# Front products of a transformer block in seven-for-eight form, and expert lists kept in DRAM

## The chip, the cores and the metric

The kernel runs on one core of one Trainium2 chip. The metric is the device time of one execution in microseconds (us): 1033.31 us as the median of 3 runs (1033.22 to 1034.61). A core has five engines with a queue of instructions each: TensorE (PE), VectorE (DVE), ScalarE (ACT), GpSimd (POOL) and SyncE (SP), which issues most DMA transfers. POOL issues the indirect ones (gathers and scatters by a list of rows).

## The reference

Sixteen sequences of 512 tokens with 256 features pass through one block, all in float32:

```python
xn = _layernorm(x, axis=-1)
x = x + attention(xn) + experts(xn)
# attention: 16 heads of 16, linear (no softmax over tokens)
q, k = elu(xn @ Wq + bq) + 1, elu(xn @ Wk + bk) + 1;  v = xn @ Wv + bv
kv = einsum('bkhd,bkhm->bhdm', k, v)
out = einsum('bqhd,bhdm->bqhm', q, kv) / max(sum over tokens of q.k, 1e-6) @ Wo + bo
# experts: one shared, and 2 of 8 routed
shared = swiglu(xn @ w_in.T) @ w_out.T
g = the better of 2 groups by softmax(xn @ wg.T + gb)
e_logits = xn @ we.T + eb, softmax inside group g; the best two of its 4 experts
h = swiglu(xn @ w1.T)                      # 512 wide, common to all experts
routed = sum over the two of weight * (h @ w2[e].T)
```

The two experts of a token are in the same group of four, so a token has one of 12 pairs.

## The kernel before, in words

**Sequences.** The loop over `b` handles one sequence of 512 tokens (4 tiles of 128) in an iteration. It also runs the front of sequence b+1 and the normalization of sequence b+2. In PE's order an iteration is: `project` of b+1 (k with the 8 + 2 logits beside it, 8 products of 266 columns on line 412, then q, 8 of 256 on line 423), `summarize` of b (L689, keys against normalized inputs), `hidden_rows` of b (L595, h in token rows, sent to `h_d` in DRAM), `key_sum` of b+1 (L679), `hidden` of b (L621, the shared expert's hidden values), the small `values` and `mix` (L708, L731), and `gather` (L768, the shared expert and attention outputs added to the residual `res`, also sent to `h_d`).

**Seven products for eight.** `hidden_rows` and `hidden` compute a 2 by 2 block product with 7 block products. `weight_sums` (L527) makes four sums of weight blocks once, `token_sums` (L538 to L541) four sums of the token blocks of each sequence, from the transposed input `xnT`. `seven` walks 14 products (7 for each of 2 halves `u`) through three PSUM banks a half, called tall, wide and lone; between products ACT copies a bank out and DVE adds others to it. A product that continues a bank waits for that copy.

**Order.** Each engine has one fixed order, made by a scheduler from the order of the text, priorities and its own estimate of times; `keep_in_program_order`, `issue_after` and `high_priority` steer it. PSUM is split into 6 banks for `ps_mm` and 2 for `ps_y`. Tiles with the same tag share buffers. SP's transfers also go out in one order.

**Front.** After the products DVE adds the biases (L416, L417, L427), `feature_map` makes elu + 1 with an exponential on ACT (L398 to L402), and `route` finds the pair of each token (L446 to L515): `hot` marks it, `ahead_of` counts, on POOL, the tokens of each pair in the same partition in earlier tiles. `attend` divides the queries by their normalizer and sends them through DRAM to be transposed (`turn`, L258 and L264).

**Sorting.** After the front of sequence 15, `order` sorts all 8192 tokens by pair into tiles of 128, each tile of one pair. It turns counts into slots, and then makes, for 8 groups of 8 token tiles, one-hot marks on DVE (L877 to L890) that 64 bfloat16 products on PE (L894) sum to the list of tokens of each tile. The result is `source` and `goal` (L921, L923). `between` runs these steps piece by piece between the products of sequences 14 and 15.

**Routed experts.** There are at most 75 tiles; 67 are done always, the rest under a condition on the count. Two tiles make a pair of tiles. `rows` (L943) gathers rows of `h_d`, 770 values each: 512 of h, 256 of the base (residual, attention and shared expert) and two weights. `turn` (L964 to L976) transposes h, `sums` multiplies by the two experts' weights (L993), adds weights and base (L1000, L1003), and scatters the rows to the output (L1006). The gathered rows live in four homes, the memory of qq_all, x_all, kk_all and xn_all. The first three pairs of tiles are gathered early for h (L943 at 768 us), and once more after the last residual rows are in `h_d`.

## Time and profile before

| | before |
|---|---|
| median of 3 runs | 1033.31 us |
| profiled execution | 1033.23 us |
| its span, first to last instruction | 1031.5 us |
| PE busy / DVE / ACT / POOL | 1004.9 / 779.4 / 488.1 / 254.8 us |
| granted PE clock, mean | 0.998 |

The profile records one execution. A row of a group gives line, engine, operation and tiles, a count, then busy time and mean duration. A float32 matrix product shows as two records. Durations of PE records overlap, so the distance between starts is what a product costs in a full queue. In rows in order of time, the bracket at the end gives idle time before the instruction and what released it. Time stamps are us from the start of the span.

### The profile page before, as it was taken

What the parts mean: (1) busy time and instruction counts of PE and PEld (TensorE: products, weight loads), DVE (VectorE), ACT (ScalarE), POOL (GpSimd) and SP (SyncE); (2) the same over time, 40 slices, a digit from 0 to 9 for tenths busy, and PEclk for the clock granted to TensorE, in tenths of its full rate; (3) what the DMA queues carried; (4) which work ended last, traced back from release to release, by engine and by line L of the source; (5) the groups of instructions that cost most, each with busy time, mean ns of one, the idle gap of its engine ahead of it and who ended that gap; (6) DMA issues with size and microseconds to landing.
All of it is one profiled execution on the core that took longest, in us unless ns stands there. A gap on an engine that the chain in (4) does not pass through costs nothing. (4 is left out here: it accounts for less than half of the span.)

```text
span 1031.5 us, 12407 instructions
## 1 busy us (share of the span) xinstructions
PE 1004.9 (97%) x3704; PEld 681.7 (66%) x3704; DVE 779.4 (76%) x1974; ACT 488.1 (47%) x893; POOL 254.8 (25%) x359
## 2 busy tenths in 40 slices
PE   7999999999999999999999999999899999999996
PEld 5466868677786868686777768686667344444442
DVE  5978687878778787878787877868975776666663
ACT  3525353535445253535343534425136576766671
POOL 5302020111202021110202020201012766555652
PEclk9999999999999999999999999999999999999999
DMA  7063534525152522314141313221235755555440
GB/s 220 16 177 107 141 104 101 147 59 154 51 163 54 161 84 81 122 42 143 37 128 56 110 55 123 72 77 61 62 110 146 225 172 153 147 156 157 150 147 30
DMA packets 130339, 116.08 MB, mean 113 GB/s; under 512 B 72637, under 2 KB 114109, under 8 KB 130272
## 3 DMA queue, kind: packets, MB, share of 16 engines
q1 hardware_dynamic: 120064, 77.43, 25.7%
q0 software_dynamic: 9392, 37.58, 12.2%
q8 instruction: 31, 0.51, 0.2%
q10 hardware_dynamic: 816, 0.27, 0.2%
q14 instruction: 36, 0.29, 0.1%
HBM read 65.36 MB, written 50.27 MB: 112 GB/s over the span
## 5 line engine op out<-in xcount | busy, mean ns | idle before, releaser
L993 PE MATMUL py<-w_sb,hT 128*128 x536 | 230.7, 592 | 1.7 <-DVE hT L976 1.6
L993 PEld LDWEIGHTS py<-w_sb,hT 128*128 128x128 f32 x536 | 101.7, 190 | 130.1 <-issue 129.1
L768 PE MATMUL po<-wout_sb,hs_all 128*128 128x256 f32 x480 | 116.6, 380 | 1.4 <-DVE hs_all L580 1.4
L390 POOL TENSOR_TENSOR res<-x_all,bo_sb 128x256 f32<-128x256 f32 x64 | 48.5, 792 | 274.4 <-DMA h_d<-res 203.4
L768 PEld LDWEIGHTS po<-wout_sb,hs_all 128*128 128x128 f32 x480 | 89.2, 190 | 15.1 <-DVE hs_all L580 3.4
L1006 POOL DMA_INDIRECT out<-y,goal x67 | 67.8, 1012 | 76.3 <-DVE y L1003 65.3
L676 POOL TENSOR_TENSOR k<-kk_all 128x512 f32<-128x512 f32 x16 | 20.9, 1307 | 258.3 <-DVE sm L458 247.7
L777 DVE TENSOR_TENSOR res<-po,res 128x256 f32<-128x256 f32 x60 | 25.4, 424 | 76.6 <-PE po L768 76.5
L398 ACT ACTIVATE km<-km 128x1024 f32<-128x1024 f32 x16 | 16.9, 1057 | 138.7 <-DVE km L397 134.4
L595 PE MATMUL phr_w<-w_sb,ss 128*128 128x512 f32 x120 | 61.5, 594 | 2.2 <-DVE ss L538 1.9
L768 PE MATMUL po<-kvo,qT 128*128 128x256 f32 x240 | 61.7, 383 | 0.0
L621 PE MATMUL phs_w<-ss,win_sb 128*128 128x256 f32 x240 | 61.6, 379 | 0.0
L621 PE MATMUL phs_t<-xnT,win_sb 128*128 128x256 f32 x240 | 61.6, 379 | 0.0
L595 PE MATMUL phr_t<-w_sb,xnT 128*128 128x512 f32 x120 | 61.3, 593 | 0.0
L595 PE MATMUL phr_t<-w_sb,ss 128*128 128x512 f32 x120 | 59.4, 597 | 0.0
L621 PE MATMUL phs_t<-ss,win_sb 128*128 128x256 f32 x240 | 59.1, 379 | 0.0
L689 PE MATMUL pxk<-kk_all,xn_all 128*128 128x256 f32 x256 | 58.0, 379 | 0.0
L412 PE MATMUL pk<-wkr_sb,xnT 128*128 128x266 f32 x240 | 57.2, 387 | 0.0
L423 PE MATMUL pq<-w_sb,xnT 128*128 128x256 f32 x240 | 54.2, 379 | 0.0
L689 PEld LDWEIGHTS pxk<-kk_all,xn_all 128*128 128x128 f32 x256 | 48.5, 190 | 6.7 <-issue 0.2
L964 ACT COPY hb<-qq_all 32x256 f32<-32x256 f32 x108 | 43.4, 402 | 17.1 <-DMA qq_all<-h_d,source 9.7
L412 PEld LDWEIGHTS pk<-wkr_sb,xnT 128*128 128x128 f32 x240 | 45.4, 190 | 8.0
(216 smaller groups left out, 1966.0 us busy)
## 6 DMA issues: line engine op xcount, KB each, us to landing
h_d<-hr SPq DMA_DIRECT2D x64, 256.0 KB, 2.5
q_d<-qq_all SPq DMA_DIRECT2D x16, 512.0 KB, 2.8
qb<-q_d SPq DMA_DIRECT2D x64, 128.0 KB, 3.1
w_sb<-in_w SPq DMA_DIRECT2D x64, 128.0 KB, 3.5
h_d<-res SPq DMA_DIRECT2D x60, 129.0 KB, 1.9
x_all<-in_x SPq DMA_DIRECT2D x15, 512.0 KB, 4.8
xn_d<-xn_all SPq DMA_DIRECT2D x14, 512.0 KB, 3.9
xb<-xn_d SPq DMA_DIRECT2D x56, 128.0 KB, 2.8
```

The costliest lines, as they stand in the source:

```text
L390: nc.gpsimd.tensor_tensor(res[:, t, 0:D], xt[:, t, :], bo_sb, ALU.add)
L412: nc.tensor.matmul(pk, lhsT=xnT[:, k, ts(t, P)], rhs=wkr_sb[:, k, :], start=(k == 0), stop=(k == KD - 1),)
L423: nc.tensor.matmul(pq[:, t, :], lhsT=xnT[:, k, ts(t2 + t, P)], rhs=wq_sb[:, k, :], start=(k == 0), stop=(k == KD - 1),)
L595: tc.keep_in_program_order(nc.tensor.matmul(to, lhsT=xs7[i][:, ts(u, P)], rhs=w1_in[W7[i]], start=start, stop=stop, skip_group_check=True,))
L621: tc.keep_in_program_order(nc.tensor.matmul(split(to)[:, f, :], lhsT=win_in[W7[i]][:, ts(2 * u + f, P)], rhs=xs7[i], start=start and f == ...
L676: nc.gpsimd.tensor_tensor(k2, kk[:, 0:2, :], kk[:, 2:4, :], ALU.add)
L689: nc.tensor.matmul(pxk[:, c, :], lhsT=xn[:, t, ts(c, P)], rhs=kk[:, t, :], start=(t == 0), stop=(t == NT - 1),)
L768: nc.tensor.matmul(po, lhsT=a, rhs=w, start=(i == 0), stop=(i == len(parts) - 1))
L777: nc.vector.tensor_tensor(res[:, t, 0:D], po, res[:, t, 0:D], ALU.add)
L964: nc.scalar.copy(there[ts(q, Q), a - near, 0:n, :], self.hg[ts(a, Q), 0:n, ts(q, W)])
L993: nc.tensor.matmul(py.rearrange("p j d -> p (j d)"), lhsT=self.hT[:, f, ts(j, P)], rhs=w2_sb[:, f, bass.ds(regs[i % TR], 2 * D)], start=(f ...
L1006: stored = nc.gpsimd.indirect_dma_start(out=out_rows, out_offset=bass.IndirectOffsetOnAxis(ap=self.goal[:, i : i + 1], axis=0), in_=y, in_ ...
```

## The change

**Front products.** From sequence 2 on `project7` replaces `project`. It computes k and q together by 14 products of 261 columns: the k side has 256 columns of k, the four logits of group 0 and its group logit, the q side the same with group 1. ACT copies and DVE adds take the results out of PSUM. The query bias is then added by DVE and the key bias by POOL. `token_sums` runs at the end of the iteration before and serves `project7`, `hidden_rows` and `hidden`. The weight blocks `kq_sb` are loaded at the start, completed with the logit columns by POOL copies (`by_side`) and summed by DVE (`weight_sums`) in iteration 0.

**Lists.** `clear_lists` fills a list in DRAM for each pair in iteration 0 (780 rows of 4096 bytes). `enlist` finds, for each sequence, each token's place in its pair's list with two bfloat16 products, and scatters the token numbers, one entry of 32 bytes for a token, with four scatters. `order` is reduced to the counts; it gathers the tiles' lists from DRAM with one gather and transposes them on PE. The marks, their 64 products and `between` go.

**Rows.** A row has 771 values: h, weights, base, and one of padding. Thus its last third (257 values) is a row of its own for `bases`, which fetches the final base for the first three pairs instead of a second whole gather. `hs_all` becomes a fifth home, and rows are gathered four pairs ahead. Buffers of kvo, y and ss have new tags. `values` and `mix` of sequence 14 are placed between the products of `hidden`, as those of sequence 15, and its outputs start with the attention part.

```diff
-    BASE = D + 2
...
+    BASE = 2 + D + 1
     ROW = HID + BASE
+    LAST = D + 1
...
+    kq_sb = wp.tile([P, SEVEN, SIDE], FP)
+    kq_in = [kq_sb[:, i, :] for i in range(SEVEN)]
+    kq_12 = w2_sb[:, 0, 2 * D : 2 * D + SIDE]
+    nc.sync.dma_start(out=kq_sb[:, 0:KD, 0:D], in_=wk.rearrange("(p c) f -> p c f", p=P))
+    for k, to in enumerate((kq_12, kq_in[2])):
+        nc.sync.dma_start(out=to[:, 0:D], in_=wq.rearrange("(p c) f -> p c f", p=P)[:, k])
+    bl_sb = const.tile([P, G, EL], FP)
+    def by_side():
+        for g, y in enumerate((kq_in[0:2], (kq_12, kq_in[2]))):
+            for to, rows in [*((y[k], wkr_sb[:, k]) for k in range(KD)), (None, bkr_sb)]:
+                to = bl_sb[:, g, :] if to is None else to[:, D:SIDE]
+                nc.gpsimd.tensor_copy(to[:, 0:EG], rows[:, D + g * EG : D + (g + 1) * EG])
+                nc.gpsimd.tensor_copy(to[:, EG:EL], rows[:, D + E + g : D + E + g + 1])
...
         res = work.tile([P, NT, BASE], FP, tag="res", name=f"res_{b}")
         xt = xs.pop(b)
         for t in range(NT):
-            nc.gpsimd.tensor_tensor(res[:, t, 0:D], xt[:, t, :], bo_sb, ALU.add)
+            nc.gpsimd.tensor_tensor(res[:, t, 2 : 2 + D], xt[:, t, :], bo_sb, ALU.add)
+        nc.gpsimd.memset(res[:, :, 2 + D :], 0.0)
         return res
...
+    def project7(b, xs7):
+        sides = [a[:, b % 2] for a in (kk_all, qq_all)]
+        kk, qq = sides
+        tall, wide, lone = [None] * 2, [None] * 2, [None] * 2
+        for u in range(2):
+            tall[u], wide[u], lone[u] = (
+                ps_mm.tile([P, SIDE], FP, tag="mm", name=f"pkq_{b}_{u}_{i}") for i in "twl"
+            )
+        for u, i in (
+            (0, 1), (0, 5), (1, 1), (0, 6), (1, 5), (1, 6), (0, 7), (0, 2), (1, 7), (0, 4), (1, 2),
+            (0, 3), (1, 4), (1, 3),
+        ):
+            to = lone[u] if i == 2 else wide[u] if i in (3, 5) else tall[u]
+            tc.keep_in_program_order(nc.tensor.matmul(
+                to, lhsT=xs7[i - 1][:, ts(u, P)], rhs=kq_in[W7[i - 1]],
+                start=i in (1, 2, 5), stop=i in (2, 3, 4), skip_group_check=True,
+            ))
+            a1, b1, a2, b2 = kk[:, u, :], qq[:, u, :], kk[:, 2 + u, :], qq[:, 2 + u, :]
+            with tc.high_priority():
+                if i in (1, 6, 7, 4):
+                    last_copy[:] = [nc.scalar.copy({1: a1, 6: b1, 7: b2, 4: a2}[i], tall[u])]
+                if i in (7, 2, 3):
+                    c, p = {7: (b2, wide[u]), 2: (a1, lone[u]), 3: (b1, wide[u])}[i]
+                    nc.vector.tensor_tensor(c, c, p, ALU.add)
+        lg = small.tile([P, NT, G * EL], FP, tag="lg", name=f"lg_{b}")
...
+        for y, bias, tag, engine in (
+            (qq, bq_sb, "qm", nc.vector), (kk, bkr_sb[:, 0:D], "km", nc.gpsimd),
+        ):
+            engine.tensor_tensor(
+                y[:, :, 0:D], y[:, :, 0:D], bias.unsqueeze(1).to_broadcast([P, NT, D]), ALU.add
+            )
+            feature_map(b, y, tag)
+        return qq[:, :, 0:D], kk[:, :, 0:D], lg
...
+    def clear_lists():
+        free = work.tile([P, P * WORDS], U32, tag="blocks", name="free")
+        nc.gpsimd.memset(free, FREE)
+        R = lists_d.shape[0]
+        for r in range(0, R, P):
+            n = min(P, R - r)
+            nc.sync.dma_start(out=lists_d[r : r + n, :], in_=free[0:n, :])
...
+    def enlist(b):
+        pr = ps_y.tile([P, NT, NP], FP, tag="py", name=f"pr_{b}")
+        flat = pr.rearrange("p t c -> p (t c)")
+        mine = hot[:, ts(b, NT), :]
+        nc.tensor.matmul(flat, lhsT=before, rhs=mine.rearrange("p t c -> p (t c)"), start=True, stop=False)
+        nc.tensor.matmul(
+            flat, lhsT=ones_bf, rhs=ahead_of[:, ts(b, NT), :].rearrange("p t c -> p (t c)"),
+            start=False, stop=True,
+        )
+        rk = small.tile([P, NT, NP], FP, tag="rk", name=f"rk_{b}")
+        nc.vector.tensor_tensor(rk, pr, lists_at.unsqueeze(1).to_broadcast([P, NT, NP]), ALU.add)
+        nc.vector.tensor_tensor(rk, rk, mine, ALU.mult)
+        rf = small.tile([P, NT], FP, tag="rf", name=f"rf_{b}")
+        nc.vector.tensor_reduce(rf, rk, AX.X, ALU.add)
+        spot = small.tile([P, NT], U32, tag="spot", name=f"spot_{b}")
+        nc.vector.tensor_scalar(spot, rf, float(WORDS), None, ALU.mult)
+        for t in range(NT):
+            put = nc.gpsimd.indirect_dma_start(
+                out=entries,
+                out_offset=bass.IndirectOffsetOnAxis(ap=spot[:, t : t + 1], axis=0),
+                in_=ids[:, b * NT + t : b * NT + t + 1], in_offset=None,
+            )
+            tc.declare_no_dep(put.ins, group="lists", reason="every token has an entry of its own")
+            tc.add_to_no_dep_group("lists", put.ins)
...
         (x11, x12), (x21, x22) = halves(xnT)
-        ss = one.tile([P, 4, S // 2], FP, tag="ss", name=f"ss_{b}")
...
-        if b + 1 == B:
+        if b + 2 >= B:
...
-        with tc.high_priority() if b + 1 == B else nullcontext():
+        kvo = one.tile([P, KD, D], FP, tag="xk", name=f"kvo_{b}")
+        with tc.high_priority() if b + 2 >= B else nullcontext():
...
             nc.tensor.matmul(po, lhsT=a, rhs=w, start=(i == 0), stop=(i == len(parts) - 1))
         return po
...
+        past = keep.tile([P, NP - 1], FP)
+        nc.vector.tensor_scalar(past, starts[:, 1:], row, None, ALU.is_le)
+        nc.vector.tensor_tensor(past, past, jump[:, 0 : NP - 1], ALU.mult)
+        begin = keep.tile([P, 1], FP)
+        nc.vector.tensor_reduce(begin, past, AX.X, ALU.add)
+        part = keep.tile([P, 1], U32)
+        nc.vector.tensor_scalar(part, begin, row, 1.0 / P, ALU.add, ALU.mult)
+        got = work.tile([P, P * WORDS], U32, tag="blocks", name="got")
+        nc.gpsimd.indirect_dma_start(
+            out=got[0:TILES, :], out_offset=None, in_=lists_d,
+            in_offset=bass.IndirectOffsetOnAxis(ap=part[0:TILES, :], axis=0),
+        )
+        tokens = keep.tile([P, P], FP)
+        nc.vector.tensor_copy(
+            tokens[0:TILES, :], got[0:TILES, :].rearrange("p (n w) -> p n w", w=WORDS)[:, :, 0]
+        )
         yield
...
-        def marks(g):
-            row_of, tile_of = (place_of[:, i, ts(g, TG)].unsqueeze(2) for i in range(2))
-            lo, hi = los[:, g % 4], his[g % 3]
-            nc.vector.tensor_tensor(
-                lo, count.unsqueeze(1).to_broadcast([P, TG, P]), row_of.to_broadcast([P, TG, P]),
-                ALU.is_equal,
-            )
-            at_tile = one.tile([P, TG, TILES], BF, tag="at_tile", name=f"at_tile_{g}")
-            nc.vector.tensor_tensor(
-                at_tile, count[:, 0:TILES].unsqueeze(1).to_broadcast([P, TG, TILES]),
-                tile_of.to_broadcast([P, TG, TILES]), ALU.is_equal,
-            )
-            nc.vector.tensor_tensor(
-                hi[:, :, 0, :], at_tile,
-                number[:, ts(g, TG)].unsqueeze(2).to_broadcast([P, TG, TILES]), ALU.mult,
-            )
-            nc.vector.tensor_scalar(hi[:, :, 1, :], at_tile, row, None, ALU.mult)
...
-        def add(g):
-            for t in range(TG):
-                tc.keep_in_program_order(nc.tensor.matmul(
-                    pi, lhsT=los[:, g % 4, t, :], rhs=his[g % 3][:, t].rearrange("p i n -> p (i n)"),
-                    start=(g + t == 0), stop=(g * TG + t == TT - 1),
-                ))
...
+        pi = ps_y.tile([P, TILES], FP, tag="py", name="pi")
+        nc.tensor.transpose(pi, tokens[0:TILES, :], ident[0:TILES, 0:TILES])
...
+        def bases(self):
+            for j, i in enumerate(self.tiles):
+                nc.gpsimd.indirect_dma_start(
+                    out=self.hg[:, j, HID + 2 :], out_offset=None,
+                    in_=h_d.rearrange("r (a w) -> (r a) w", w=LAST),
+                    in_offset=bass.IndirectOffsetOnAxis(ap=lasts[:, i : i + 1], axis=0),
+                )
...
         res = residual(b)
-        qq, kk, lg = project(b, xnT)
-        route(b, lg, res)
+        qq, kk, lg = project7(b, sums7[b]) if b in sums7 else project(b, xnT)
...
-            steps_of_order = order()
         if b + 1 == B:
-            sums7 = token_sums(b, xnT)
-            hidden_rows(b, sums7, {2: 2, 6: 2, 9: 2, 13: 2}.get)
+            hidden_rows(b, sums7[b])
             for e in waiting:
                 load_expert(e)
-            *lists, filled = next(steps_of_order)
             tiles = [Tiles(list(range(i, min(i + 2, SURE))), *lists) for i in range(0, SURE, 2)]
+            lasts = keep.tile([P, 2 * AHEAD], U32)
+            parts = ROW // LAST
+            nc.vector.tensor_scalar(
+                lasts, lists[0][:, 0 : 2 * AHEAD], float(parts), float(parts - 1), ALU.mult, ALU.add
+            )
...
         if b + 1 < B:
             sums = key_sum(b + 1, fronts[b + 1][2])
             queries[b + 1] = attend(b + 1, fronts[b + 1][1], sums)
-        if b + 2 == B:
-            next(steps_of_order)
+        if 0 < b < B - 1:
+            enlist(b + 1)
         if b + 1 == B:
             for w in tiles[:AHEAD]:
                 w.rows()
-        if b + 1 < B:
-            hs, made = hidden(b, sums7) if b else first_hidden(xnT)
+        if b + 2 < B:
+            hs, made = hidden(b, sums7[b]) if b else first_hidden(xnT)
+            if b == 0:
+                clear_lists()
+                by_side()
+                for _ in weight_sums(kq_in, kq_12):
...
             made_of = {}
-            hs, made = hidden(b, sums7, then)
+            hs, made = hidden(b, sums7[b], then)
             kvo = made_of["kvo"]
-        if b + 2 == B:
-            next(steps_of_order)
         if b + 1 == B:
             for i, w in enumerate(tiles[: AHEAD - 1]):
                 w.turn(made[i])
             gather_last(b, res, qT, kvo, hs)
         else:
...
-            gather(b, res, qT, kvo, hs, normed[b + 2][2]() if b + 2 < B else None, {0: 2, 1: 2, 3: 2}.get)
+            if b + 2 == B:
+                steps_of_order = order()
+                next(steps_of_order)
+            last = gather(b, res, qT, kvo, hs, normed[b + 2][2]() if b + 2 < B else None)
+            if b == 0:
+                with tc.issue_after(last.ins):
+                    sums7[1] = token_sums(1, normed[1][1])
+            if b + 2 < B:
+                sums7[b + 2] = token_sums(b + 2, normed[b + 2][1])
+            if b + 2 == B:
+                *lists, filled = next(steps_of_order)
...
-    for w in tiles[: AHEAD - 1]:
+    EARLY = len(rows_of) - 1
+    for w in tiles[AHEAD:EARLY]:
         w.rows()
     for g, w in enumerate(tiles):
-        if g + AHEAD < len(tiles):
-            tiles[g + AHEAD].rows()
+        if g + EARLY < len(tiles):
+            tiles[g + EARLY].rows()
         if g + AHEAD - 1 < len(tiles):
             tiles[g + AHEAD - 1].turn()
         if g == 0:
-            tiles[AHEAD - 1].rows()
+            for v in tiles[:AHEAD]:
+                v.bases()
         w.sums()
```

## The prediction

> **What bounds the kernel now.** I read the totals first, then stretches of the span, then what TensorE (PE) waited for, then its instructions in order of time. Totals of the page, and busy time by stretch (columns: stretch, its length, then busy PE, weight loads, DVE, ACT, POOL with counts, PE clock, DMA share, GB/s); the first is one steady sequence, the last is most of the routed experts at the end:
>
> ```profile
> PE 1004.9 (97%) x3704; PEld 681.7 (66%) x3704; DVE 779.4 (76%) x1974; ACT 488.1 (47%) x893; POOL 254.8 (25%) x359
> ```
> ```profile
> 311.04:358.48 47.44, 47.44 (x195) 35.97 (x194) 37.43 (x97) 21.30 (x31) 6.90 (x11) 1.00 0.41 112
> ```
> ```profile
> 720.00:766.00 46.00, 41.06 (x206) 29.96 (x205) 45.09 (x79) 11.14 (x19) 0.00 (x0) 1.00 0.18 57
> 766.00:790.00 24.00, 24.00 (x117) 21.24 (x116) 14.31 (x32) 15.43 (x34) 5.80 (x6) 1.00 0.71 188
> 790.00:812.50 22.50, 20.91 (x50) 9.06 (x49) 9.95 (x24) 10.21 (x26) 13.41 (x14) 1.00 0.65 210
> 812.50:1022.00 209.50, 209.40 (x488) 92.26 (x486) 139.06 (x335) 143.37 (x360) 118.59 (x120) 1.00 0.49 147
> ```
>
> PE is the bound and at its full clock: a steady sequence has no idle PE at all, so there only less PE work, or a new wait, moves the time. The exception is 720 to 766, where the tokens are sorted by expert pair: DVE is busy 45.1 of 46 us, PE lacks 4.9. PE's list of waits says whose they are:
>
> ```profile
> PE pm L731 <- DVE rz L748: 2.5, 1, 2.5
> PE phr_w L595 <- DVE ss L538: 1.9, 1, 1.9
> PE py L993 <- DVE hT L976: 1.6, 1, 1.6
> ```
>
> The first two, with 0.3 for hr L574 and 0.2 for qq_all L890, make 4.9 us of sorting; the third lies at 812, where rows of the fourth tile pair came late. The remaining waits lie at the start.
>
> **The change, part by part.**
>
> *Products of k, q and logits.* PE in order of time (start, length, what):
>
> ```profile
> 311.04 3.76 PE L412 MATMUL pk<-wkr_sb,xnT 128*128 128x266 f32 x16
> 314.64 3.61 PE L423 MATMUL pq<-w_sb,xnT 128*128 128x256 f32 x16
> 318.09 3.62 PE L689 MATMUL pxk<-kk_all,xn_all 128*128 128x256 f32 x16
> ```
>
> A float32 product shows as two records, so the 8 of pk take 314.64 - 311.04 = 3.60 us, 0.450 each at 266 columns; the 8 of pq 3.45, 0.431 at 256. Together 7.05 us. The new form has 14 products of 261 columns: halfway, 0.4405 each, 6.17 us. That is 0.88 us for each of 14 sequences (2 to 15): **-12.3 us**. It's a gain only while PE stays full. In the trace each engine's order isn't that of the text (batch statistics of a later sequence run between the key adds), so that the two token sums needed first should fill DVE's idle 2.2 us between the last two residual adds (L777), ahead of the products; they take 4 x 0.42.
>
> *New waits inside those 14 products.* The third use of a bank must wait until ACT has copied the first. A product's result reaches ACT 0.20 us after its 0.44 (phs_t at 336.67, copied at 337.73 after two products of 0.43); the copy has the row of L338, 128x256 in 372 ns; PE continued 0.07 after such a copy (324.05 to 324.12). That is 1.08 us against the 3 x 0.44 = 1.32 at which (0,6) comes due: covered by 0.24, as ACT idles for some 10 us there (11.18 before L398). The weakest DVE link is (0,3), which needs the add after (0,7): its copy ends 3.66 us after the start, the add of 0.42 at 4.2, and (0,3) is due at 4.85. If ACT or DVE were held by one more 1.06 us operation, PE would lose 0.4 to 0.8.
>
> *What moves between engines, each sequence.* DVE loses four key adds (0.42), four logit adds (0.16) and two query adds (0.69), 3.7 us; it gains six adds from PSUM (0.42), two small ones (0.17), a query bias add of 1024 (row L750, 1.22) and four small ones for the lists (0.17): 4.8. Net +1.1, 38.5 of a 46.7 us sequence. ACT gains 8 copies, 3.0 us of 26 idle. POOL gains the key bias add and four scatters (row L1006, 1.01 and 0.3 between: 5.2 us). All three have room. The key add's price: L676 takes 1307 ns for 512 and L677 809 for 256, so 1024 take some 2.3 to 2.6 us.
>
> Here a rule of the Trainium skill speaks against the change. "SBUF — State Buffer", section "SBUF: two separate sides": VectorE and GpSimd have one port pair in common, which is locked for a whole instruction; a VectorE operation with two SBUF inputs, or in a two-port mode, waits for a GpSimd operation to end. The rows agree: the tiny product of L467 runs beside L676.
>
> ```profile
> 320.26 1.31 POOL L676 TENSOR_TENSOR k<-kk_all 128x512 f32<-128x512 f32 x1 [37.64 <-DVE sm L458]
> 320.60 1.02 DVE L467 TENSOR_TENSOR pe<-ex,sm 128x32 f32<-128x32 f32 x1
> ```
>
> L489 has the same shape and takes 0.19; L467 ended as POOL did. By rows of unhindered work alone, the key add costs nothing (POOL is idle 85%). By the rule, DVE loses up to 2.4 us more just before the hidden rows' evacuations, and the key chain (POOL, minimum on DVE, exponential on ACT 1.06) comes some 3 us later than now. ACT works in order: counted from the first front product, phr's first result is there at 6.17 + 3.46 + 0.86 + 0.2 = 10.7, its fourth product is due at 12.2, and the 0.58 us copy between has 0.9 to spare; the exponential may sit before it. DVE reaches L574 with 0.2 us idle in this sequence (1.28 at 423, in a later one) and PE needs it 1.1 after that. So the stall is 0 to 1.5 us a sequence; I take 0.25, near the low end because two thirds of the 2.4 us fall into idle DVE time: 14 x 0.25 = **+3.5 us** (0 to +21).
>
> *Lists.* Each of 16 sequences gets two bfloat16 products of 48 columns on PE. The nearest row is the sorting product of 150 columns: eight fit between 738.65 and 739.19, 0.067 each.
>
> ```profile
> 738.65 0.70 PE L894 MATMUL pi<-kk_all,x_all 128*128 128x150 bf16 x8
> 739.19 1.50 PE L768 MATMUL po<-wout_sb,hs_all 128*128 128x256 f32 x6
> ```
>
> 32 x 0.067 = **+2.1 us**. The skill's "TensorE: Matmul & The Clock Gate", section "Wait — 56ns, not 53.3ns?", puts the floor of a small matmul at about 25 ns, which would make an estimate of 0.8; the weights change each time here, so I take the row. The 64 scatters of 128 four-byte entries are hidden: nothing reads them before sequence 14. Clearing the lists writes 3.2 MB in sequence 0; at 512 KB in 2.8 to 4.8 us that is 18 to 30 us of the SP queue. Behind it stand residual rows, experts and the queries of sequence 1, needed some 40 us later; without that cover the delay would reach PE, 0 to 5, taken as 0.
>
> *Sorting goes.* 64 products of 0.067, -4.3 us; the float32 counts of L813 and L815 against one small product and one transpose, 0. Eight times 3.1 us of DVE marks and 6 us of other sorting disappear, and sequence 14 gets its value products placed inside the hidden products as 15 has now: **-4.3 - 4.9 = -9.2 us**. New: the lists come back by a gather. Sequence 15's entries are written after its query scaling: from 716, about 4 us of DVE work, four scatters to 726, landing 3.0 later, gather 1.0 and 3.9 (row of h_d gathers): 735, before PE's residual products now end (744, after the change some 739). The transpose stands behind those, so a stall of 0 to 4; **+0.5**.
>
> *Start.* The seven weight blocks of k and q are built in sequence 0: twelve POOL copies (row L474, 0.22) and four DVE subtractions (0.42), due at 72 when sequence 2's products begin. POOL is idle from 46.5 to 76.9, but the clearing memset shares a buffer that is free only at 70.6 (L264). If the copies queue behind it, PE waits some 3 us; **+1.5** (0 to 3). The added 0.5 MB of weight loads come last, tens of us before use.
>
> *End.* Three gathers of whole rows a second time become last-third gathers, still 1.25 us of POOL each, and a fifth home lets the fourth pair's rows go first: 795 instead of 800. They land 5 us earlier, against a stall of 1.6: **-1.6 us**. The first y then waits for its base until about 804 rather than 799; PE owns six banks of 3.43 us, to 810, so that's covered. The remaining 209 us are PE alone and stay.
>
> **Sum.** -12.3 + 3.5 + 2.1 - 9.2 + 0.5 + 1.5 - 1.6 = -15.5 us. The profiled execution took 1033.2 with a span of 1031.5, the median is 1033.3; so span 1016 and time **1017.8 us**.
>
> **Rivals.**
>
> 1. *PE stalls in every front part*: product banks or the port lock hold ACT or DVE. Place: L574 and L567 of each sequence. For it: DVE's 0.2 us of room at 328 and the lock; against: 9.5 us of idle DVE in the same sequence. It turns the change slower from (15.5 + 3.5)/14 = 1.36 us of stall a sequence; at 2 us the time is 1033.3 - 19 + 28 = 1042.
> 2. *The milder form*, 0.6 to 1.2 us a sequence: the first seven for eight is eaten, sorting's gain is left: 1033.3 - 19 + 12.6 = 1027.
> 3. *The 14 products save nothing*, as each might cost its fixed part: then 1030 with small stalls. Against it: 266 and 256 columns already differ by 4%.
> 4. *The list chain comes late* for the transpose, 4 us and more: 1022. It lies within my range.
>
> **Chances.** Forecast, 1010 to 1022: 0.60; milder stalls or no product gain, 1022 to 1031: 0.17; within 0.2% (2.1 us, about what a measurement of this kernel can tell): 0.04; slower by rival 1: 0.18; under 1010: 0.01. Faster is 0.78. The forecast's own range is 1010 to 1022; eight in ten need the upper cases to 1034.
>
> **What would show it.** Steps between one pk product of a sequence and the next of 46.6 to 47.0 us instead of 47.4; 6.2 us of front products; no PE wait for ACT copies of the new product or for r_phr; POOL's 1024 add at 2.3 us and beside it stretched DVE work; no PE wait between 700 and 750 over 0.5; no wait at the eighth tile. Wrong if the sequences take over 48 us, whatever happens at the end.

## The result and the profile after

The kernel became slower: a median of 1060.04 us (1059.46 to 1060.43, 4 runs) beside 1033.67 us for the kernel before (1033.22 to 1034.61). The ratio on record is 1.0251, its 95% interval 1.0238 to 1.0264. The forecast was 1017.8 us in a range of 1010 to 1022, or up to 1034 with its milder stalls. The profiled execution took 1060.4 us with a span of 1058.7; before it was 1033.2 and 1031.5.

First the totals of the kernel after.

```profile
PE 998.7 (94%) x3614; PEld 667.1 (63%) x3614; DVE 779.1 (74%) x1991; ACT 520.0 (49%) x999; POOL 359.4 (34%) x468
```

PE (TensorE) is busy 1004.9 - 998.7 = 6.2 us less than before, and the span is 27 us longer: idle PE grew from 26.6 to 60.0 us. The forecast's terms take 12.3 + 4.3 - 2.1 = 14.5 us of work off PE, so 8.3 us of that saving are missing in the busy time too; they are there in a kernel without the new waits (below). Busy time by stretch of the kernel after (columns: stretch, length, then busy PE, weight loads, DVE, ACT, POOL with counts, PE clock, DMA share, GB/s); the first is one steady sequence, the last two are the end:

```profile
534.39:583.61 49.22, 47.21 (x193) 35.26 (x192) 38.49 (x100) 23.10 (x39) 13.59 (x17) 1.00 0.30 86
730.00:812.00 82.00, 80.52 (x328) 60.17 (x327) 53.73 (x137) 40.07 (x73) 16.34 (x18) 1.00 0.40 110
812.00:1045.00 233.00, 230.51 (x539) 102.14 (x537) 149.41 (x361) 154.15 (x387) 132.26 (x134) 1.00 0.49 145
1045.00:1059.00 14.00, 0.00 (x0) 0.00 (x0) 0.00 (x0) 0.00 (x0) 0.00 (x0) 0.53 0.02 8
```

A sequence of before in this part of the kernel took 47.76 us with 0.28 of idle PE; now there are 2.0 us of it:

```profile
556.25:604.01 47.76, 47.48 (x196) 35.94 (x195) 37.67 (x98) 20.18 (x30) 6.45 (x11) 1.00 0.30 89
```

The stretch of the sorting (720 to 790 before) has become dense: 1.5 us idle in 82. And at the end stand 14 us in which no engine is busy. Before, that stretch was half as long:

```profile
1024.00:1032.00 8.00, 0.00 (x0) 0.00 (x0) 0.00 (x0) 0.00 (x0) 0.49 (x1) 0.66 0.04 13
```

To place the 27.2 us, I take the first record of the state product (pxk) of sequences 2 and 14, the first expert product (py), and the end of POOL's last indirect write instruction in each trace:

| stretch | before | after | difference | forecast |
|---|---|---|---|---|
| up to pxk of sequence 2 | 128.35 | 132.25 | +3.9 | +0.5 |
| pxk of 2 to pxk of 14, 12 sequences | 570.76 | 598.17 | +27.4 | -6.0 |
| pxk of 14 to the first py | 90.73 | 81.90 | -8.8 | -8.7 |
| first py to the end of the last write | 234.7 | 232.5 | -2.2 | -1.6 |
| last write to the end of the span | 7.0 | 13.9 | +6.9 | none |

(-6.0 is 12 times -0.88 + 0.25 + 0.13; +0.5 is the forecast's start term of 1.5 with two such sequences, since the front products of 2 and 3 run before that point.) The sorting and the experts did what the forecast said. Three rows did not. The start is 3.4 us over. The sequences take 49.85 us on average instead of 47.56; one of them, from 431.5 us, took 53.6, with 2.2 us of wait before the key sum (pks) and a granted clock of 0.50 from 448.6 to 452.0. And there is a stretch behind the last write that the forecast doesn't have.

What PE waited for in the kernel after (total, times, longest):

```profile
PE phr_t L706 <- ACT r_phr L678: 20.4, 14, 1.5
...
PE pkq_w L478 <- DVE ss L649: 3.8, 6, 1.5
PE pks L790 <- POOL k L788: 3.2, 2, 2.2
PE phs_t L732 <- ACT r_phs L678: 2.4, 2, 1.5
PE phr_t L706 <- ACT hr L681: 2.0, 5, 0.6
```

The first line is the new one: in each of the 14 sequences PE stands about 1.5 us before the fourth of the hidden rows' products (phr), because ACT hasn't yet copied the first out of its bank. The sorting's own waits of before (rz 2.5, ss 1.9) and the one at the eighth tile (hT 1.6) are gone. PE and ACT of one sequence, in order of time (start, length, what; in brackets the idle time before it and its releaser):

```profile
528.22 0.60 PE L478 MATMUL pkq_t<-kq_sb,xnT 128*128 128x261 f32 x2
...
534.39 0.38 PE L800 MATMUL pxk<-kk_all,xn_all 128*128 128x256 f32 x1
...
537.85 1.02 PE L706 MATMUL phr_t<-w_sb,xnT 128*128 128x512 f32 x2
...
542.07 1.13 PE L706 MATMUL phr_t<-w_sb,ss 128*128 128x512 f32 x2 [1.48 <-ACT r_phr L678]
```
```profile
537.99 1.06 ACT L431 ACTIVATE qm<-qq_all 128x1024 f32<-128x1024 f32 x1 [1.85 <-DVE qq_all L498]
539.07 1.28 ACT L534 ACT_TABLE_LOAD   x1
540.36 0.24 ACT L534 ACTIVATE ex<-ex 128x40 f32<-128x40 f32 x1
540.50 1.04 ACT L432 ACTIVATE qm<-qm 128x1024 f32<-128x1024 f32 x1
541.45 0.56 ACT L678 COPY r_phr<-phr_t 128x512 f32<-128x512 f32 x1
```

The 14 front products take 534.39 - 528.22 = 6.17 us, the forecast's number to the digit. The fourth phr product was due at 540.42 (537.85 and three steps of 0.86) and came at 542.07, and the one behind it 0.96 later instead of 0.86. The copy that it needs stands on ACT behind the whole feature map of q: two passes of 1.06, a table load of 1.28 and the gate's exponential. The chain begins one engine earlier, on DVE and POOL:

```profile
535.11 1.71 DVE L491 TENSOR_TENSOR lg<-qq_all,bl_sb 128x20 f32<-128x20 f32 x1
536.74 1.21 DVE L498 TENSOR_TENSOR qq_all<-qq_all,bq_sb 128x1024 f32<-128x1024 f32 x1
```
```profile
534.61 2.17 POOL L498 TENSOR_TENSOR kk_all<-kk_all,bkr_sb 128x1024 f32<-128x1024 f32 x1 [1.01 <-ACT kk_all L485]
```

The tiny logit sum L491, whose twin on kk_all takes 0.18 us half a microsecond before, lasts 1.71 and ends as POOL's key bias ends: the port lock that the forecast named, with a price of 1.5 us. In the kernel before, the key map was a thing of the past at this point. Its exponential on ACT, and PE's pxk in that sequence:

```profile
554.41 1.06 ACT L398 ACTIVATE km<-km 128x1024 f32<-128x1024 f32 x1 [8.91 <-DVE km L397]
...
559.39 1.06 ACT L401 ACTIVATE qm<-qm 128x1024 f32<-128x1024 f32 x1
```
```profile
556.25 3.62 PE L689 MATMUL pxk<-kk_all,xn_all 128*128 128x256 f32 x16
```

It began 1.84 us before pxk, while PE still made the query products; in the kernel after, it comes at 543.86, 9.5 us behind pxk. In between lies the form of the change itself: keys and queries are finished together, by the last two of 14 products, where before the keys were finished after 8 of 16.

The lines of the last drain of GpSimd's queue (durations least/median/longest in ns, then first and last start), in the kernel after and in the one before:

```profile
L1247 POOLq DRAIN  x3: 51/103/8727, 1049.1 to 1058.4; - x3
```
```profile
L1161 POOLq DRAIN  x3: 51/103/3418, 1027.2 to 1031.2; - x3
```

It has grown by 5.3 us. That is most of the 6.9 us behind the last write; the other 1.6 lie between that write and this drain (2.7 us before, 4.3 after).

### The profile page after: what moved, and what is told of

Same layout as the page of the kernel before. It is cut to its first block, busy times and chain, and to the rows that moved or that the text cites. A ratio compares the mean times of both kernels' runs of the same rounds, so it can differ in the third digit from the quotient of the medians.

```text
span 1058.7 us, 12513 instructions
## 1 busy us (share of the span) xinstructions
PE 998.7 (94%) x3614; PEld 667.1 (63%) x3614; DVE 779.1 (74%) x1991; ACT 520.0 (49%) x999; POOL 359.4 (34%) x468
## 5 line engine op out<-in xcount | busy, mean ns | idle before, releaser
L625 POOL DMA_INDIRECT lists_d<-ids,spot x64 | 67.0, 1047 | 135.5 <-DVE spot L623 109.7
L878 PEld LDWEIGHTS po<-wout_sb,hs_all 128*128 128x128 f32 x480 | 89.9, 190 | 14.1 <-DVE hs_all L691 2.7
L419 POOL TENSOR_TENSOR res<-x_all,bo_sb 128x256 f32<-128x256 f32 x64 | 52.1, 842 | 124.4 <-DMA h_d<-res 116.8
L485 ACT COPY kk_all<-pkq_t 128x261 f32<-128x261 f32 x56 | 21.1, 377 | 140.0 <-PE pkq_t L478 139.1
L706 PE MATMUL phr_t<-w_sb,ss 128*128 128x512 f32 x120 | 60.9, 610 | 22.5 <-ACT r_phr L678 20.4
L498 POOL TENSOR_TENSOR kk_all<-kk_all,bkr_sb 128x1024 f32<-128x1024 f32 x14 | 30.5, 2176 | 122.0 <-ACT kk_all L485 111.6
L706 PEld LDWEIGHTS phr_t<-w_sb,ss 128*128 128x128 f32 x120 | 21.2, 190 | 58.1 <-ACT r_phr L678 32.3
L732 PEld LDWEIGHTS phs_t<-ss,win_sb 128*128 128x128 f32 x240 | 45.3, 190 | 9.0 <-ACT r_phs L678 3.1
L878 PEld LDWEIGHTS po<-kvo,qT 128*128 128x128 f32 x240 | 44.5, 190 | 10.2 <-ACT kvo L847 4.7
```

The costliest lines, as they stand in the source:

```text
L419: nc.gpsimd.tensor_tensor(res[:, t, 2 : 2 + D], xt[:, t, :], bo_sb, ALU.add)
L485: last_copy[:] = [nc.scalar.copy({1: a1, 6: b1, 7: b2, 4: a2}[i], tall[u])]
L498: engine.tensor_tensor(y[:, :, 0:D], y[:, :, 0:D], bias.unsqueeze(1).to_broadcast([P, NT, D]), ALU.add)
L625: put = nc.gpsimd.indirect_dma_start(out=entries, out_offset=bass.IndirectOffsetOnAxis(ap=spot[:, t : t + 1], axis=0), in_=ids[:, b * NT + ...
L706: tc.keep_in_program_order(nc.tensor.matmul(to, lhsT=xs7[i][:, ts(u, P)], rhs=w1_in[W7[i]], start=start, stop=stop, skip_group_check=True,))
L732: tc.keep_in_program_order(nc.tensor.matmul(split(to)[:, f, :], lhsT=win_in[W7[i]][:, ts(2 * u + f, P)], rhs=xs7[i], start=start and f == ...
```

## The experiments

Three causes could make the r_phr wait: the lock of POOL's key bias; the square root of the batch statistics, which the change orders behind the last front copy, with its table load; or the bunching of both maps itself, however they are spread. Each ratio below is to the kernel before, measured beside it. "A sequence" is the mean step of pxk from sequence 2 to 14.

### The lock, the order behind the copies, and both

```diff
-            (qq, bq_sb, "qm", nc.vector), (kk, bkr_sb[:, 0:D], "km", nc.gpsimd),
+            (qq, bq_sb, "qm", nc.vector), (kk, bkr_sb[:, 0:D], "km", nc.vector),
```

> The kernel after, with the bias of the keys (L498's second turn, 128x1024 on GpSimd beside VectorE's qq) on VectorE. Sequences of after take 49.85 us on average between the products of the state, those of before 47.56. Theory 1 (port lock: GpSimd's 2.17 us on SBUF stretch VectorE's logits sum L491 to 1.71 us, the query bias comes 1.5 us late, and with it ScalarE's first copy of the row products): L491 falls to about 0.2 us, the wait of the row products on ScalarE's L678 falls from 20.4 us to 1 to 4, the sequences to about 48.0, the time to 1033 to 1038. Theory 2 (it is ScalarE's table load that stands in front): the stall stays above 1 us a sequence and the time at 1048 or more.

```diff
-                    last_copy[:] = [nc.scalar.copy({1: a1, 6: b1, 7: b2, 4: a2}[i], tall[u])]
+                    nc.scalar.copy({1: a1, 6: b1, 7: b2, 4: a2}[i], tall[u])
```

> The kernel after, with the copies of the seven products no longer put ahead of the norm's Sqrt (project7's last_copy is not set). Theory 1 (port lock alone): the table load of Exp leaves the front part, but the query bias is still late; the wait on L678 stays at 16 to 20 us and the time at 1054 to 1060. Theory 2 (the table load): 14 loads of 1.28 us leave the way of the first copy, the wait falls to 3 to 6 us and the time to 1040 to 1045.

> Both edits together: the key bias on VectorE, and the Sqrt not held behind the copies. If these two are the whole of the stall, the wait of the row products on L678 is under 2 us, the sequences take 47.2 to 47.8 us and the time is 1026 to 1032 (the predicted 1017.8 plus about 7 us of GpSimd's last drain, L1247, which takes 8.7 us for 3.4 before, plus what is left of other waits). If the seven products themselves cost more than counted, the sequences stay over 48.5 us and the time over 1042.

Measured: 1068.90 us, ratio 1.0340 (1.0323 to 1.0357) with the key bias on DVE; 1059.62, 1.0249 (1.0231 to 1.0266) without the order; 1080.05, 1.0443 (1.0425 to 1.0460) with both. PE's waits with the key bias on DVE, and L491 there:

```profile
PE pks L790 <- POOL k L788: 26.0, 14, 2.4
PE phs_t L732 <- ACT r_phs L678: 7.9, 6, 1.6
...
PE phr_t L706 <- ACT r_phr L678: 0.6, 2, 0.3
```
```profile
533.56 0.17 DVE L491 TENSOR_TENSOR lg<-qq_all,bl_sb 128x20 f32<-128x20 f32 x1
```

The lock is real: without POOL's add L491 is 0.17 us, and the wait falls from 20.4 to 0.6. But the run doesn't show the lock alone, because ACT's order changed with the edit. The copy L678 now goes ahead of q's second pass:

```profile
537.27 0.24 ACT L534 ACTIVATE ex<-ex 128x40 f32<-128x40 f32 x1
537.42 0.57 ACT L678 COPY r_phr<-phr_t 128x512 f32<-128x512 f32 x1
537.88 1.06 ACT L432 ACTIVATE qm<-qm 128x1024 f32<-128x1024 f32 x1
```

Counted from the first front product (525.65 here), the copy ends 1.45 us earlier than in the kernel after. Only 0.52 of that comes from ACT's earlier start, since the key's bias now takes 1.22 us of DVE; 0.93 is the new order. That the lock's 1.5 us are as long as the wait (1.48) speaks for it as what set the wait, but no run takes the lock away and nothing else.

The kernel also got slower by 9 us. PE's order changed too: the small key-sum product pks moved four products forward, and PE now stands 2 us there for a key map that is as late as ever (its exponential starts 9.6 us behind pxk). The order behind the copies is no cause: without it the wait is 20.8, the exponential's table load stays where it was, and the time is level. The load itself was taken out in no run; there are three loads a sequence in both kernels. All this points away from the wait of one engine, to a late product of two maps, for which PE stands wherever the order lets it first.

### The lists alone

The change with the old products (16 float32 instead of 14, old weights) and its lists, gathers and fifth home:

```diff
-        qq, kk, lg = project7(b, sums7[b]) if b in sums7 else project(b, xnT)
-        route(b, b in sums7, lg, res)
+        qq, kk, lg = project(b, xnT)
+        route(b, False, lg, res)
```

> The kernel after with project in place of project7 for every sequence: the front part of before, without the seven products, their weight sums and side by side weights; token lists in DRAM, fifth home of rows and the new order at the end are kept. If all of the loss in the sequences comes from the front part: sequences of 47.5 to 47.7 us, the stretch from the last state to the first output product near 82 us (90.7 before), the last drain 8.7 us, and a time of 1026 to 1031. If the lists' scatters or the row copies slow the sequences too, they take 48.5 us or more and the time is 1040 or more.

Measured: 1035.56 us, ratio 1.0020 (1.0013 to 1.0028); a sequence 47.98 us, 47.90 in the later ones, where before has 47.76.

```profile
PE phr_w L691 <- DVE hr L670: 1.4, 5, 0.4
```

The later sequences pay 0.14 for the two list products and their restart. The earlier ones pay 0.8 (48.2 for 47.4), about 0.3 of it the wait shown; the rest wasn't traced. Up to pxk of sequence 2 the lists cost 2.9 us, and from pxk of 14 to the first py they save 10.6; the end of the span has the same 14.1 us behind the last write. So the lists alone are about level. The seven-for-eight form costs 1060.0 - 1035.6 = 24.5 us, 1.87 a sequence (49.85 - 47.98). It saved 0.88 of products in each, so its new waits cost **2.75 us a sequence**. Of these, about 2.1 are idle PE (2.31 a sequence beside 0.25 with the lists alone). The other 0.7 lengthen PE's busy time: records on both sides of a wait overlap less, and one sequence has the lowered clock.

### The stretch behind the last write

The kernel before, with 64 or 32 indirect writes of 128 four-byte entries to a tensor that nobody reads:

```diff
+            put = nc.gpsimd.indirect_dma_start(
+                out=entries,
+                out_offset=bass.IndirectOffsetOnAxis(ap=ids[:, b * NT + t : b * NT + t + 1], axis=0),
+                in_=ids[:, b * NT + t : b * NT + t + 1], in_offset=None,
+            )
```

> The kernel before with nothing but 64 more indirect writes on GpSimd (128 entries of 4 bytes each, to a scratch tensor that nobody reads, four a sequence where the lists' are). Theory 1 (GpSimd's last drain grows with the indirect transfers issued): its drain goes from 3.4 to about 8.7 us, the span grows by 5 to 7 us, the sequences stay at 47.6 us: 1038.5 to 1041. Theory 2 (the longer end of after comes from its new order at the end, not from the scatters): drain 3.4 us, 1033.5 to 1034.5. If the scatters slow the sequences as well, they take 0.3 us or more longer and the time is 1043 or more.

> The same with 32 of these writes, in the eight sequences from 7 to 14. If the drain grows with the number of transfers (5.3 us for 64): about 6.0 us, and a time of 1036 to 1037.5. If it grows in a step, 3.4 or 8.7 us and 1033.7 or 1039.

Measured: 1065.96 us (1.0313, 1.0296 to 1.0331) and 1056.96 (1.0227, 1.0210 to 1.0245). The last drain with 64, and with 32:

```profile
L1181 POOLq DRAIN  x3: 51/103/8645, 1054.3 to 1063.5; - x3
```
```profile
L1179 POOLq DRAIN  x3: 51/103/6032, 1047.8 to 1054.4; - x3
```

Before issues 140 indirect transfers and drains in 3.42 us; 32 more make it 6.03, 64 more 8.65. That is 0.082 us for each added write, hundreds of microseconds after it landed. The kernel after issues 205, which by this line gives 3.42 + 65 x 0.082 = 8.7: what it shows. The time between the last write and the drain grows along, from 2.7 to 3.3 and 4.0 us. The rest of the added time is a flaw of the experiment: with no data to wait for, the writes were all issued at the start and held POOL's own work there (the first step of pxk is 76.3 us with 64 of them, and 53.5 without). From sequence 2 on the steps are 47.56 as before.

Then the same drain under cover. Both kernels start from the change, with the key bias on DVE and pks held at its place in the text; the second has an extra drain of POOL at the read of the lists, where POOL has nothing else to do:

```diff
+        tc.keep_in_program_order(nc.tensor.matmul(pks, lhsT=ones, rhs=k2[:, 0, :], start=True, stop=True))
```
```diff
-        nc.gpsimd.indirect_dma_start(
+        read = nc.gpsimd.indirect_dma_start(
...
+        with tc.issue_after(read.ins):
+            nc.gpsimd.drain()
```

> The kernel after with the key bias on VectorE as in the run that had this alone, and the product of the keys' sum (pks, L790) held in the order of the program, behind the last row product. In the run with the bias alone the waits of the row products on L678 fell from 20.4 to 0.6 us, and 26.0 us of waits of pks on GpSimd's L788 came in their place, since the planner had put pks five products earlier. If it is that place alone: no wait over 0.5 us a sequence remains, sequences of 47.3 to 47.6 us from the ninth on, a time of 1030 to 1035. If GpSimd's sum is late whatever the order is, pks waits again, or the copies of the second hidden products do, and the time stays over 1045.

> The run before this one of the same call, with one GpSimd drain more behind the read of the lists at the start of the last sequence, where GpSimd then has some 22 us with nothing to do. If the last drain takes as long as there are indirect transfers since the drain before: the new one takes 5 us or more under cover, the last one falls from 8.7 to 3.5 us or less, and the time is 5 to 6 us under that run's. If the length has another cause, nothing changes, or the time grows by what the new drain holds up.

Measured: 1049.08 us (1.0155, 1.0138 to 1.0172) and 1041.49 (1.0078, 1.0061 to 1.0095). PE's longest wait in the first, and the drains of the second:

```profile
PE phr_w L706 <- DVE hr L685: 12.9, 14, 1.0
```
```profile
L966 POOLq DRAIN  x1: 7496/7496/7496, 755.5 to 755.5; - x1
L1249 POOLq DRAIN  x3: 51/103/2824, 1036.1 to 1039.5; - x3
```

The drain in the middle takes 7.5 us that nobody waits for, the last one falls from 8.7 to 2.8, and the time by 7.6 us. That settles where the stretch behind the last write comes from, and 6.5 us of it are left, as before. It doesn't give the rule: this last drain has 141 transfers since the drain in the middle and takes 2.82, where the kernel before takes 3.42 with 140, and 140 times 0.082 would be 11.5. What such a drain works through stays open.

The first of the two kernels is 11.0 us faster than the kernel after (1049.08 for 1060.04), with ACT's copy ahead of q's second pass here as well. With pks held, the same lateness of the maps goes to a third place, 0.9 us a sequence before a product that waits for DVE.

### The maps left out, and the maps elsewhere

If the bunched maps are what PE waits for, the waits go with the maps. This kernel leaves the feature maps of q and k out from sequence 2 on, so its products are made from other numbers, at the same cost; nothing else is changed:

```diff
-            feature_map(b, y, tag)
```

> The kernel after, with the biases but without the feature maps of q and k from sequence 2 on (seven instructions a sequence on ScalarE and VectorE, L428 to L433, are left out; its drain and the rest are those of after). Theory 3: with the maps' work gone the row products no longer wait, sequences of 46.9 to 47.4 us, 1022 to 1028 us with the long drain of 8.7 us. If the fourteen products or the lists cost TensorE time of their own, the sequences stay over 48.5 us and the time over 1040.

Measured: 1028.45 us, ratio 0.9953 (0.9937 to 0.9968), the drain still 8.7. No r_phr wait is left, and a sequence is 47.62 on average. PE is busy 990.6 us, which is 14.3 less than before where the forecast's terms say 14.5: the products cost what was forecast. The time is 31.6 us under the kernel after, for 3.0 us less of ACT in a sequence (23.1 to 20.1) and 1.6 less of DVE (38.5 to 36.9), engines that have idle time. It shows the work of the maps as the cause, not yet that it can be had for nothing. The next kernel keeps them: biases on DVE behind the last hidden-row product, maps behind the last SiLU of the hidden products, key sum and attention behind the outputs, and the extra drain.

```diff
-            feature_map(b, y, tag)
-        return qq[:, :, 0:D], kk[:, :, 0:D], lg
+        return qq[:, :, 0:D], kk[:, :, 0:D], lg, (biases, features)
...
+        with tc.issue_after(silu.ins), tc.issue_after(product.ins):
+            fronts[b][3][1]()
...
+            if b:
+                sums = key_sum(b + 1, fronts[b + 1][2])
+                queries[b + 1] = attend(b + 1, fronts[b + 1][1], sums)
```

> The run with the drain in the middle (1041.5 us), with the feature maps of q and k, ready together only when the fourteen products end, taken out of the window of the row products: both biases behind the last row product's multiply on VectorE, the maps behind the last SiLU of the second hidden products, and the keys' sum with what follows from it behind those. Nothing is left out. Theory 3 (the stall isn't the lock, the table load or one place in an order, but all of both maps' work, which came together behind the products and stands ahead of the row products' copies and adds on ScalarE and VectorE): no wait over 0.5 us in a usual sequence, 46.9 to 47.3 us a sequence (before 47.56, less 0.88 of saved columns, more 0.13 for the list products and their restart), and 1015 to 1023 us, under before. If the wait only goes on to the next place (the second hidden products' copies, the products pkq behind pks), the sequences stay at 48.3 us or more and the time over 1033.

Measured: 1045.01 us, 1.0116 (1.0098 to 1.0135). The wait before phr is gone and the later sequences take 47.03, but the earlier ones 49.1. Its list of PE's waits:

```profile
PE pkq_w L478 <- DVE qq_all L488: 8.9, 6, 1.9
...
PE pks L802 <- POOL k L800: 4.5, 1, 4.5
```

In six of the early sequences DVE's front adds come late for their bank, and POOL's key sum of the last sequence stands behind the drain at the lists' read. Two more kernels move these: the key map first, the token sums ahead, the drain earlier; in the first of them the key sum stands between the third and fourth output tile, in the second behind the fourth. Against the kernel just shown:

```diff
-            for y, bias, tag, engine in maps:
+            for y, bias, tag, engine in reversed(maps):
...
+        with tc.high_priority():
+            nc.vector.tensor_tensor(s1, x21, x22, ALU.add)
...
+        if b + 2 == B:
+            with tc.issue_after(counted.ins):
+                nc.gpsimd.drain()
```

> The run with the maps behind the hidden products, mended where its trace shows new waits: k's map ahead of q's, the keys' sum and what follows between the third and the fourth tile of the output products (it stood behind the fourth, and VectorE came 1.6 us late to the adds L488 of the next fourteen products in six sequences), the sums of token halves with high priority, and the extra drain two sequences earlier (in that run it held GpSimd's key sum, and pks waited 4.5 us). Nothing is left out. Theory 3: all sequences from the third on near 47.05 us as the later ones of that run were, the last drain at about 3 us: 1016 to 1024 us, 0.9 to 1.7 % under before. If the maps' work finds no free place in a sequence, one of its waits returns at another line, the sequences are at 48 us or more, and the time is over 1030.

> The run with the maps behind the hidden products, with three things mended and its place for the keys' sum kept (behind the fourth output tile): k's map ahead of q's, the sums of token halves with high priority, the extra drain two sequences earlier. Nothing is left out. Its sequences from the ninth on took 47.03 us and those before 49.1, with 1.6 us of waits for VectorE's L488; the run with the keys' sum between the tiles took 47.7 to 52. Theory 3 (there is room in a sequence, and the early ones lost it to VectorE waiting for the last output tile ahead of the sums): 47.0 to 47.5 us from the third sequence on, 1020 to 1028 us. If the early wait is of another making (the transposed input that comes late), they stay at 49 us and the time is 1035 to 1042.

The first was a miss: 1047.09 us, 1.0135 (1.0118 to 1.0151), 47.7 in the later sequences and up to 52 in the early ones; PE waits 3.1 us for the key sum, 6.0 for residual rows behind it and 8.7 for transposed inputs. The second comes out ahead of the kernel before beside it: 1035.07 us for 1039.99, ratio 0.9956 (0.9942 to 0.9971). One of its later sequences:

```profile
558.73:605.50 46.77, 46.77 (x194) 35.22 (x193) 39.26 (x101) 24.64 (x40) 9.63 (x16) 1.00 0.33 91
```

PE is busy in all of it, with the work of the change: in such a step of before PE is busy 47.48 of 47.76 us, and 47.48 - 0.88 + 0.14 is 46.74. It was run twice more, on other chips.

> The kernel with the maps late and the sums first once more, beside the one before it, since its first run fell on the chip where before takes 1040.0 us: there it was 0.44 % under before, with 6.9 us of waits of the output products for gathered tiles. If those waits were that chip's: 1023 to 1028 us, 0.5 to 1 % under before. If they come with the kernel (TensorE is ready for the output products earlier than the gathers), they are there again and the time is 1029 to 1032.

> The kernel with the maps late and the sums first, at a time when before takes 1033.7 us again; at the other time it was 0.44 and 0.45 % under before. If its waits of the output products (6.9 and 9.6 us) came from outside as well: 1022 to 1028 us, 0.6 to 1.1 % under before. If they are its own: 1028 to 1031 us.

Measured: 0.9955 (0.9937 to 0.9973) and 0.9944 (0.9931 to 0.9958). In these three measurements the kernel before took 1040.0, 1040.8 and 1040.1 us, where it has 1033.7 to 1034.1 beside all other runs. Against those, the times of this kernel (1035.07, 1036.96, 1034.82) are no gain. So a gain of 0.5% is shown only where the kernel before itself is 6 us slower, from a cause that isn't known. Inside the kernel the gain is small since only the later half of the sequences is clean (47.6 to 48.4 in the earlier ones), and PE waits twice at the start of the experts:

```profile
PE py L1078 <- DVE hT L1061: 6.9, 2, 3.5
```

The first of the two looks like an order again: on DVE the first y stands ahead of the next tiles' transposes, and it comes 3.6 us after POOL issued the gather of its base at 791.02. No run moved it.

### The lists alone with a hidden drain

With the last drain 5.9 us shorter (8.7 to 2.8), the lists alone should take 1029.7 us, 4 less than before. Both places of the drain were run, the second one twice, and the kernel before once more by itself:

```diff
+            with tc.issue_after(counted.ins):
+                nc.gpsimd.drain()
```

> The run with the lists alone (no seven products for k, q and the logits; 1035.6 us, with a last drain of 8.7 us that left 14.1 us behind the last output's write, where before has 7.0), with one GpSimd drain more in the next to last sequence but one, which retires 52 or more of its 64 list writes early. Nothing else is changed. If the long end is nothing but that drain: 1029 to 1031 us, 0.3 to 0.4 % under before, and the list part of the change is a gain of 4 us by itself once its drain is hidden. If the lists lose it elsewhere, 1034 us or more.

> The run with the lists alone (1035.6 us, last drain 8.7 us), with the extra GpSimd drain where it was in the run with the drain in the middle: behind the read of the lists in the last sequence, before the gathers. The run that had it two sequences earlier came out level with before (1.000), on a chip where before itself took 1040.0 us for 1033.7 elsewhere, and its trace has one wait of 8.7 us of the output products (L1050) for a gathered tile, which no other run of this study has at that length. If that wait was that chip's: 1029 to 1031 us here, 0.3 to 0.4 % under before. If the lists' end cannot gain from a hidden drain, 1033 us or more.

> The lists alone with the drain at the read of the lists, once more, at a time when before takes 1033.7 us again. If the 8.7 us of waits of its first run came from outside: 1029 to 1031 us, 0.3 to 0.5 % under before, and the lists' part is a gain by itself. If they are its own, they are there again and it is level with before.

> The kernel before itself, unchanged, for its trace at the present time: in the last two calls it takes 1040.0 and 1040.8 us for 1033.7 in all others, and the runs beside it have a wait of 8.7 us of the output products that their earlier relatives have not. If that wait comes from outside the kernel, the trace of before has one of 6 to 10 us there too, with a releaser that is none of its engines, and a time near 1040. If it is the kernels' own, before has none there, and its 6 us more are spread over the span or the time is 1033 to 1035.

Measured: ratios 1.0001 (0.9993 to 1.0010), 0.9991 (0.9982 to 0.9999) and 0.9998 (0.9990 to 1.0006), beside a kernel before that took 1040 each time; by itself, in between, that kernel took 1033.73. The drain is hidden as meant (2.8 us at the end where the read is the place, 3.5 with the early one), and each run has a new wait. PE's longest in the second of them, and the one of DVE that leads to it:

```profile
PE py L1047 <- DVE hT L1030: 8.7, 1, 8.7
```
```profile
821.05 1.78 DVE L1024 STREAM_TRANSPOSE hT<-hs_all 32x256 f32<-32x256 f32 x4 [10.27 <-remote]
```

DVE stands 10.3 us before the transposes of the fifth pair of tiles, released by none of the core's engines; the rows that they read were on ACT at 803.65 already. The lists without the drain have no idle time at that place. But the kernels with an extra drain that ran beside 1033.8 (1041.49, 1045.01 and 1047.09 us) pause 0, 2.4 and 2.4 us at this pair. The six that ran beside 1040 pause 6.1 to 11.7 us, four of them with no releaser in the core. The kernel before has no such pause in its run alone. So the pause goes with the occasion, and not with the drain by itself. What it is, and whether the 6 us more of the kernel before are the same thing, stays open; with it, the worth of the lists under a hidden drain was measured as level and not as the 4 us expected.

## Why the prediction was wrong

**The failed step** is the term "+3.5", in its words "the stall is 0 to 1.5 us a sequence; I take 0.25". It was 2.75, beyond the bound. The prediction gave rival 1 1.36 us as the point from which the change is slower. It named that rival's places (L567 and L574 of before, the hidden rows' copies and adds), and its mechanism, ACT and DVE held, with the lock in it. All of this came, larger. With 14 x 2.75 = 38.5 in place of 3.5, its sum gives 1017.8 + 35.0 = 1052.8, and with the 6.9 us behind the last write 1059.7; measured 1060.0. That the sum closes to 0.3 us proves little: the 2.75 is taken from the same traces, and there is luck in the rest, since the start comes 3.4 us later than its terms say and a sequence loses 0.42 on average to the lists where 0.13 was forecast.

What went wrong inside that step was a way of counting. The prediction asked of each added piece whether it fits into idle time of its engine, and each does: ACT is 49% busy, POOL 34%. But it took the idle time of the old order, in which the key map ran beside the query products. In the new form neither k nor q is complete before the last two of 14 products. Two maps, a bias of 1024 columns for each, the gate and two table loads then become ready at once, at 534.4, with 6.0 us until the fourth phr product is due. The chain shown needs 7.6 of them: DVE's sum and bias from 535.11, ACT's map and gate to 541.5, the copy to 542.0. The prediction saw the two ends of this ("the key chain comes some 3 us later than now"; "ACT works in order") and let the exponential "sit before" the copy at 0.9 us to spare, but counted one pass on ACT where four things stood: a pass and an exponential of q, a table load, the gate. The trace of before shows most of them in that place already, in the early sequence that the prediction reads:

```profile
321.23 1.28 ACT L401 ACT_TABLE_LOAD   x1
322.52 1.06 ACT L401 ACTIVATE qm<-qm 128x1024 f32<-128x1024 f32 x1
323.48 0.57 ACT L567 COPY r_phr<-phr_t 128x512 f32<-128x512 f32 x1
```
```profile
323.26 1.02 PE L595 MATMUL phr_t<-w_sb,xnT 128*128 128x512 f32 x2
324.12 1.11 PE L595 MATMUL phr_t<-w_sb,ss 128*128 128x512 f32 x2
```

The copy ends at 324.05, and the product that needs it starts at 324.12, on time (323.26 + 0.86). The prediction took the 0.07 between them as the delay from a copy to PE. It was all the room there was in that sequence (0.88 in the later ones: 560.82 + 0.57 against 562.27), before 1.5 us of lock were added.

**The lock.** The Trainium skill's "SBUF — State Buffer", section "SBUF: two separate sides", was put against the change by the prediction, and it holds: 1.71 us for L491 beside POOL's add, 0.17 once that add is on DVE. The prediction discounted it because "two thirds of the 2.4 us fall into idle DVE time". L491 stands at the head of DVE's queue with the query's bias behind it, so the 1.5 us went through to ACT in full. Moving the add to DVE brought ACT's start only 0.52 us forward, since the work then stands on DVE itself.

**The drain** is in no term, neither of the sum nor of the rivals. The 64 scatters were called hidden because nothing reads them, and beside the later sequences they are (the lists alone pay 0.14 there). Their price comes due at the end, 0.082 us each by the runs with 32 and 64 added writes.

**What held.** The front products, 6.17 us as worked out. POOL's add of 1024, 2.17 us by an estimate of 2.3. Sorting and list chain, -8.7 by forecast and -8.8 in the trace. The end, -1.6 and -2.2. No wait at the eighth tile. The list products were put at 0.067 each by the sorting's row, with the floor of some 25 ns of the Trainium skill's "TensorE: Matmul & The Clock Gate", section "Wait — 56ns, not 53.3ns?", beside it; the trace has them 0.03 apart:

```profile
552.04 0.19 PE L612 MATMUL pr<-hot,before 128*128 128x48 bf16 x1
552.07 0.18 PE L613 MATMUL pr<-ahead_of,ones_bf 128*128 128x48 bf16 x1
552.10 1.11 PE L732 MATMUL phs_t<-xnT,win_sb 128*128 128x256 f32 x4
```

So the floor was nearer for the product itself, but the next float32 product takes 1.11 where its like takes 1.03, and both together are the 0.14 a sequence that the lists show alone, 0.13 in the forecast. The start was mis-sized as well, +3.9 for +0.5; the lists alone cost 2.9 there. The rivals "products save nothing" and "the list chain comes late" are out by these numbers.

**The signs.** "Wrong if the sequences take over 48 us" was met, at 49.85, and "no PE wait for r_phr" failed in 14 of 14. The forecast's step of 46.6 to 47.0 exists: it is reached in the later sequences of the kernel with its maps moved (46.77), so the saving was there, and the late work around it took it back.

## What to carry to other kernels

When a change makes two results final together that were final one after the other, lay out everything that becomes ready at that moment on one line of time, per engine in its order, against the next thing that the bound engine needs; idle shares and the gaps of the old order say nothing of it. A wait that disappears when one cause is taken away has only been moved if the time doesn't fall: look where the same work is awaited next, and whether an engine's order changed with the edit, before calling it a cure. And look at GpSimd's last drain when a kernel gets more indirect transfers: here each added write cost 0.082 us there, and an earlier drain in idle time of GpSimd took this away.

## What was unexpected of the hardware

The last drain of GpSimd's queue took 3.42 us after 140 indirect transfers, 6.03 after 172, 8.65 after 204 and 8.73 after 205, although those added had landed hundreds of microseconds earlier. After a drain in the middle (7.50 us, behind 64 transfers) it took 2.82 with 141 transfers more, so the number since the last drain doesn't set it alone. And beside a kernel before that took 1040 us, DVE stood 6.1 to 11.7 us in four kernels, at the fifth pair of tiles, with no releaser among the core's engines; the cause is open.
